# Two cross-attention layers: one maximum and one subtraction a step for the scores of both layers, image scores read from the score tile by ScalarE

## The chip, the cores and the metric

One Trainium2 chip, one core of it. The metric is the device time of one execution, in microseconds (us); the kernel before took 2496.99 us, the median of three runs (2496.69 to 2499.29). Four compute engines work side by side: TensorE (PE, its weight loads are PEld), VectorE (DVE), ScalarE (ACT) and GpSimd (POOL). SyncE (SP) issues most DMAs. TensorE writes its results to PSUM, eight banks; ScalarE and VectorE read them there.

## What is computed

64 sequences of 256 tokens with 320 channels go through two cross-attention layers with 20 heads of 16 channels each. The context has 77 tokens of 512 channels. Layer 0 uses all 77 as text (the reference's image part of layer 0 is over an empty slice). Layer 1 uses the first 73 as text and the last 4 as image tokens:

```python
# layer 0
q, k, v = heads(x @ Wq.T), heads(text @ Wk.T), heads(text @ Wv.T)
x = softmax(q @ k.T * scale) @ v  -> @ Wo.T + bo + x
# layer 1
probs_t = softmax(q @ k_t.T * scale)              # 73 text tokens
attn    = q @ k_ip.T * scale                      # 4 image tokens
qsem    = l2norm(probs_t @ text_ehs)
fused   = attn + 0.5 * (qsem @ l2norm(ip_ehs).T)
ip_out  = (softmax(fused) * mask) @ v_ip
x = (probs_t @ v_t + ip_out) @ W_out + b_out + x
```

A softmax does not change when the same number is taken from all scores of a row, so any number near the maximum may be subtracted. `fused` is shifted by its own maximum later, in `image_shifted`.

## The kernel before

All 64 sequences are taken in 32 pairs p. A pair has ten units of attention in each layer: for each of its two sequences five (part, half) units, each of 128 tokens by eight heads. The main loop goes over steps g; k = g mod 10 is the place in a pair's ten. Step g works on three units at once:

- the scores of layer 0 of unit g and of layer 1 of unit g - 13 (`now[0]`, `now[1]`),
- the transposes of the weights of the units before (`last0`, `last1`),
- layer 1's "semantics" of the unit before that (`before1`): sums over the text with values, Gram matrix and ones.

One PSUM tile `sc` of four banks [128, 4, 512], a single buffer, holds all scores of a step. Each bank has 2 x 77 columns for layer 0, 2 x 77 for layer 1 and, from column 308, 2 x 94 for the semantics. `scores` (L659) and `semantics` (L774, L781) write it. The next step's L774 may begin only when this step's readers are through. Two more PSUM pools have two banks each: `ptr` (tag "tr") for transposes, `pms` (tag "ms") for projections, keys, values, Gram matrices and attention times values. A buffer is taken over when the copy that empties it has ended. These copies are nearly all ScalarE's.

The order of a step, engine by engine, is the order in which the loop issues it (`keep_order` fixes that from step 13 on):

- TensorE: L774, L781, L659; transposes of layer 1 (`tr` L723, `rtr` L724); a filler; transposes of layer 0; more fillers; `attend` (`pv` L809, L814) in steps 0, 2, 5 and 7.
- VectorE: for each layer a maximum (L677) and a subtraction (L679) by `shifted`; `prod` (L792, L795) by `weighted`; the sum (L705) and reciprocal (L706) by `normalize`; `nrm` (L1130).
- ScalarE: copies of what earlier fillers left in PSUM; `pt`, `pr` of layer 1 (L730, L731); the exponential of layer 0 (L687), in step 5 after layer 0's `pt`; the first fillers' copies, such as keys `kT` (L348), values `vs` (L391), Gram (L516, L517), last queries (L589); `pt`, `pr` of layer 0 (L738, L741, L749, L750); the copy of the sums (L1057) by `sums_out`, ahead of layer 0's `pt` in steps 1, 6 and 8; the two exponentials of layer 1 (L690, L691); the second fillers' copies.
- GpSimd: the copy of layer 1's four image scores out of `w` (L694); the normalisation of layer 0 (`parts`, L710); masks and placing.

Fillers that matter here: step 0 the Gram matrix `g_ps`, and `attend`; step 2 `q_ps` L575 and `attend`; step 4 keys `k_ps` and two query tiles `q_ps` (L547); step 5 `k_ps` and `attend`; step 6 a pair of value rows `v_ps`; step 7 `k_ps`, `kl_ps` and the transposes of the image weights `itr` (L915, `image_transposed`), then `attend`; step 8 value rows, then `outputs` with `atr` and `ltr`, of which `ltr` sits in the transposes' pool.

`place_image_keys` (step 6) puts the four image keys behind the 73 text keys of layer 1, in columns 73 to 76; `keys_by_head` spreads keys over a block by head (`kbd`).

Of the kernel before, what the change touches and what calls it, by code (L numbers as in the profile page):

```python
# [8 lines left out]
F32 = mybir.dt.float32  # L9
AF = mybir.ActivationFunctionType  # L10
ALU = mybir.AluOpType
AX = mybir.AxisListType
# [7 lines left out]
T = 77  # L20
NIP = 4
TT = T - NIP
P = 128
KE = E // P
PAD = 32
# [4 lines left out]
GR = GV - M  # L30
R0, R1 = T - M, TT - M
QR = 32
# [38 lines left out]
def tile_two_cross_attentions(ctx: ExitStack, tc: tile.TileContext, a: dict, out: bass.AP):  # L71
# [35 lines left out]
    nc = tc.nc  # L107
# [15 lines left out]
    def load_chan(name, queue):  # L123


        w = const.tile([P, 4, C], F32, tag=name, name=name)
        nc.vector.memset(w[HALF:, 2, :], 0.0)
        nc.vector.memset(w[:HALF, 3, :], 0.0)
        queue.dma_start(w[:, :2, :], a[name][: 2 * P, :].rearrange("(i p) c -> p i c", p=P))
        for b in range(2):  # L130
            queue.dma_start(w[b * HALF : (b + 1) * HALF, 2 + b, :], a[name][2 * P :, :])
        return w

    def load_out(name, queue):
        w = const.tile([P, 4, C], F32, tag=name, name=name)
        nc.vector.memset(w[HALF:, 2, :], 0.0)
# [198 lines left out]
    kTs, kbds, qs, aTs = {}, {}, {}, {}  # L335

    def keys(l, p, i):

        nt = (T, TT)[l]
        if i == 0:  # L340
            kTs[l] = big.tile([P, 2, 2, T], F32, tag=f"kT{l}", name=f"kT{l}_{p}", bufs=1)
        ps = pms.tile([P, 512], F32, tag="ms", name=f"k_ps{l}_{p}_{i}")
        pv = ps[:, : 2 * nt].rearrange("p (b t) -> p b t", b=2)
        for k in range(KE):
            nc.tensor.matmul(  # L345
                pv, wk[l][:, k, i * P : (i + 1) * P], cts[p][:, k, :, :nt], start=(k == 0), stop=(k == KE - 1)
            )
        nc.scalar.copy(kTs[l][:, i, :, :nt], pv)  # L348

    def last_keys(p):  # L350

        ps = pms.tile([P, 512], F32, tag="ms", name=f"kl_ps{p}")
        pv = ps[:, : 2 * T].rearrange("p (b t) -> p b t", b=2)
        for k in range(KE):
            nc.tensor.matmul(pv, wk_last[:, k, :], cts[p][:, k], start=(k == 0), stop=(k == KE - 1))
        for l in range(2):
            nt = (T, TT)[l]
            kl = kls[l, p] = big.tile([P, 2, T], F32, tag=f"kl{l}", name=f"kl{l}_{p}", bufs=1 + l)
            own, other = (slice(h * HALF, (h + 1) * HALF) for h in (l, 1 - l))
            nc.scalar.copy(kl[own, :, :nt], pv[own, :, :nt])  # L360
            nc.sync.dma_start(kl[other, :, :nt], kl[own, :, :nt])

    kls = {}

    def place_image_keys(p):

        k = kipT[:, :, 2 * p * NIP : 2 * (p + 1) * NIP].rearrange("p i (b t) -> p i b t", b=2)
        nc.gpsimd.tensor_copy(kTs[1][:, :, :, TT:], k[:, :2])
        nc.gpsimd.tensor_copy(kls[1, p][:, :, TT:], k[:, 2])

    def keys_by_head(l, p, b):

        kbd = kbds[l, b] = big.tile([P, 3, 2, T], F32, tag=f"kbd{l}", name=f"kbd{l}_{p}_{b}")
        for i, k in ((slice(0, 2), kTs[l][:, :, b, :]), (slice(2, 3), kls[l, p][:, b : b + 1, :])):
            full = [P, k.shape[1], 2, T]
            nc.gpsimd.tensor_tensor(
                kbd[:, i], k.unsqueeze(2).broadcast_to(full),
                head_mask[:, :2].unsqueeze(1).unsqueeze(3).broadcast_to(full), ALU.mult,
            )
# [33 lines left out]
    def values(l, p, b):  # L413

        nt = (T, TT)[l]
        rem = nt - M
# [225 lines left out]
    stats = {}  # L642
    ws, pts = {}, {}

    def eight(t, u):

        return t[:, PLACES[u] : PLACES[u] + 8].rearrange("p (r e) ... -> p r e ...", e=2)

    SEM0 = 4 * T

    def scores(ps, start, stop, l, p, b, u):

        part, s = UNITS[l][u]
        q, kbd, t0 = qs[l, p, part], kbds[l, b], b * S + s * P
        tokens = q[:, b, :] if part == 2 else q[:, t0 : t0 + P]
        for r in range(4):
            rows = slice(r * QR, (r + 1) * QR)
            for c in halves_of(P):
                nc.tensor.matmul(  # L659
                    ps[c, r, 2 * T * l : 2 * T * (l + 1)], tokens[rows, c],  # L660
                    kbd[rows, part].rearrange("p e t -> p (e t)"), start=start, stop=stop,
                )

    def shifted(ps, l, p, b, u):


        nt = (T, TT)[l]
        name = f"{l}_{p}_{b}{u}"
        if l and u == 0:
            stats[p, b] = (  # L670
                small.tile([P, 2 * H, NIP], F32, tag="att", name=f"att{p}_{b}", bufs=3),
                big.tile([P, 2 * H, NIP + D + 1], F32, tag="sums", name=f"sums{p}_{b}", bufs=3),
                small.tile([P, 2 * H], F32, tag="nrm", name=f"nrm{p}_{b}", bufs=3),
            )
        sc = ps[:, :, 2 * T * l : 2 * T * (l + 1)].rearrange("p r (e t) -> p r e t", t=T)
        mx = small.tile([P, 4, 2], F32, tag="mx", name=f"mx{name}")
        nc.vector.tensor_reduce(mx, sc[:, :, :, :nt], AX.X, ALU.max)  # L677
        w = ws[l] = sp.tile([P, 4, 2, T], F32, tag=f"w{l}", name=f"w{name}", bufs=2 - l)
        nc.vector.tensor_tensor(  # L679
            w, sc, mx.unsqueeze(3).broadcast_to([P, 4, 2, T]), ALU.subtract  # L680
        )

    def exponential(l, g, p, b, u):

        w = ws[l]
        if not l:
            nc.scalar.activation(w, w, AF.Exp, scale=SCALE)  # L687
            return
        two = ws[l] = parts1[g % 3]
        nc.scalar.activation(two[:, :4].rearrange("p (e a) j t -> p (a j) e t", e=2), w[:, :, :, :M], AF.Exp, scale=SCALE)  # L690
        nc.scalar.activation(  # L691
            rests(two), w[:, :, :, M:TT], AF.Exp, scale=SCALE
        )
        nc.gpsimd.tensor_copy(eight(stats[p, b][0], u), w[:, :, :, TT:])  # L694

    def rests(two):

# [3 lines left out]
    def normalize(g):  # L701

        w = ws[0]
        sm = small.tile([P, 4, 2], F32, tag="sm", name=f"sm{g}")
        nc.vector.tensor_reduce(sm, w, AX.X, ALU.add)  # L705
        nc.vector.reciprocal(sm, sm)  # L706
        two = ws[0] = sp.tile([P, 8 * T], F32, tag="parts0", name=f"parts0_{g}")
        w, sm = (t.rearrange("p j g ... -> p (j g) ...") for t in (w, sm))
        for t0, t1 in ((0, M), (M, T)):
            nc.gpsimd.tensor_tensor(  # L710
                two[:, 8 * t0 : 8 * t1].rearrange("p (h t) -> p h t", h=8), w[:, :, t0:t1],
                sm.unsqueeze(2).broadcast_to([P, 8, t1 - t0]), ALU.mult,
            )

    def transposed(l, p, b, u, w):
# [47 lines left out]
    def semantics(ps, start, stop, p, b, u, rows):  # L763
# [5 lines left out]
        for i in range(4):  # L769
            for j in range(2):  # L770
                half_rows = slice(j * M, (j + 1) * M)
                at = SEM0 + i // 2 * GV
                for c in halves_of(P):
# [91 lines left out]
    full = [P, 2 * H, NIP]  # L865
# [195 lines left out]
    for g in range(NP * NU + LAG + 12):  # L1061
        p, k = divmod(g, NU)
# [4 lines left out]
        now = [unit(g), unit(g - LAG)]  # L1067
        ps = prod = None
# [5 lines left out]
        if now[0] or now[1] or before1:  # L1074
            ps = psc.tile([P, 4, 512], F32, tag="sc", name=f"sc{g}")
# [6 lines left out]
            for n, (fn, args) in enumerate(todo):  # L1082
                fn(ps, n == 0, n == len(todo) - 1, *args)
        ends = before1 and before1[2] == BU - 1
        for l in range(2):
            if now[l]:
                shifted(ps, l, *now[l])
        if g in middle:
            fn, args = middle.pop(g)
            fn(*args)  # L1090
# [1 line left out]
        if last1:  # L1092
            transposed(1, *last1)
            new1 = (*last1, pts[1])
        if now[0] and k != 5:
            exponential(0, g, *now[0])
        if k == 2:
# [4 lines left out]
        if k != 2:  # L1102
            for fn, args in first:
                fn(*args)
        if before1 and k in (1, 6, 8):
            sums_out(ps)
        if last0:
            transposed(0, *last0)
# [6 lines left out]
            keep_busy(8)  # L1115
        if now[0] and k == 5:
            exponential(0, g, *now[0])
        if before1 and k not in (1, 6, 8):
            sums_out(ps)
        for fn, args in between.pop(g, ()):  # L1120
            fn(*args)
# [6 lines left out]
        if before1:  # L1128
            q, b, u = before1[:3]
# [10 lines left out]
        if last0:  # L1140
            q, b, u, _ = last0
# [9 lines left out]
        before1 = new1  # L1151
# [52 lines left out]
```

## Time and profile before

| | us |
|---|---|
| runs, median (lowest to highest) | 2496.99 (2496.69 to 2499.29) |
| profiled execution, own time | 2497.88 |
| its span, first to last instruction | 2496.2 |
| mean granted TensorE clock | 0.997 |

The costliest groups of VectorE and ScalarE around the change, from the table of groups kept apart by shape:

| line | what | count | mean ns |
|---|---|---|---|
| L677 | maximum, 616 numbers, layer 0 | 320 | 796 |
| L677 | maximum, 584 numbers, layer 1 | 320 | 756 |
| L679 | subtraction, 616 numbers | 640 | 800 |
| L792, L795 | `prod`, 512 and 72 numbers | 320 each | 681, 223 |
| L687 | exponential of layer 0, 616 numbers | 320 | 719 |
| L730 | `pt`, 512 numbers | 320 | 585 |
| L731 | `pr`, 128 numbers | 320 | 273 |
| L1057 | sums, 168 numbers | 320 | 300 |
| L694 | image scores on GpSimd, 32 numbers | 320 | 210 |

In such lines "128x616" is partitions by elements; "x320" counts instructions; the idle time in square brackets or after the bar is the engine's own just before the instruction, with what ended it. A row of the list of waits has the total in us, the number of times and the longest. Printed times of instructions that follow each other on an engine overlap by about 0.1 us, since the next one starts before the last result is written.

### The profile page before, as it was taken

How to read it: one execution, taken by the hardware profiler on the slowest of the kernel's cores; microseconds unless marked ns; L12 is line 12 of the kernel's file. 1: busy time of each engine (PE TensorE's matmuls, PEld its weight loads, DVE VectorE, ACT ScalarE, POOL GpSimd, SP SyncE). 2: the span in 40 equal slices, each digit the busy share in tenths (PEclk: the TensorE clock that was granted, in tenths of full speed). 3: DMA queues.
4: the chain of work that ended last, by engine and by line, in shares of the span. 5: the costliest groups of instructions: out<-in, count | busy, mean ns of one | idle time of the engine just before them, and what ended most of it. 6: DMA issues, size and time to landing. Idle time of an engine off the chain costs nothing.

```text
span 2496.2 us, 100470 instructions
## 1 busy us (share of the span) xinstructions
PE 2401.9 (96%) x41118; PEld 1849.4 (74%) x41118; DVE 1987.1 (80%) x3673; ACT 1479.6 (59%) x3767; POOL 1371.7 (55%) x3483
## 2 busy tenths in 40 slices
PE   8899999999999999999999999999999999999888
PEld 5677777777777777777777777777777777777666
DVE  3588888888887888888888888888887888888764
ACT  3465666665665665665665666665665666666543
POOL 2456555556555656555555555555555556555542
PEclk9999999999999999999999999999999999999999
DMA  5212111112211121211111211111211111211000
GB/s 172 75 30 58 55 53 47 48 53 60 59 47 46 48 58 56 61 45 46 48 58 55 63 43 50 44 58 55 63 43 50 44 58 55 61 39 39 26 23 25
DMA packets 150914, 131.83 MB, mean 53 GB/s; under 512 B 45432, under 2 KB 129144, under 8 KB 150456
## 3 DMA queue, kind: packets, MB, share of 16 engines
q1 hardware_dynamic: 149592, 124.27, 17.2%
q8 instruction: 325, 5.32, 0.9%
q10 hardware_dynamic: 864, 1.15, 0.2%
q14 instruction: 133, 1.09, 0.1%
HBM read 87.43 MB, written 33.91 MB: 49 GB/s over the span
## 4 chain that ended last, share of the span: by engine, by line
PE 75%; DVE 15%; ACT 4%; DMA 2%; issue 2%; POOL 1%; SPq 0%; DVEq 0%; POOLq 0%; ACTq 0%
PE sc L774 9%; PE tr L723 9%; PE o_ps L547 8%; PE q_ps L547 8%; PE sc L659 7%; DVE w L679 6%; DVE mx L677 4%; PE sc L781 4%; PE o_ps L632 3%; PE k_ps L345 3%; PE pv L809 3%; PE v_ps L390 2%; PE o_ps L557 2%; DVE prod L792 2%; PE q_ps L557 2%; PE q_ps L575 2%
## 5 line engine op out<-in xcount | busy, mean ns | idle before, releaser
L677 DVE TENSOR_REDUCE mx<-sc 128x8 f32<-128x584 f32 (+1 forms) x640 | 496.9, 776 | 365.1 <-PE sc L659 362.2
L710 POOL TENSOR_TENSOR parts<-w,sm 128x512 f32<-128x512 f32 (+1 forms) x640 | 440.5, 709 | 459.8 <-DVE sm L706 184.0
L679 DVE TENSOR_TENSOR w<-sc,mx 128x616 f32<-128x616 f32 x640 | 512.0, 800 | 73.0 <-DVE mx L677 0.9
L723 PE MATMUL tr<-ident,parts 128*128 128x128 f32 x2560 | 408.1, 282 | 9.5 <-ACT pt L730 5.6
L723 PEld LDWEIGHTS tr<-ident,parts 128*128 128x128 f32 x2560 | 284.7, 141 | 128.7 <-issue 83.2
L730 ACT COPY pt<-tr 128x512 f32<-128x512 f32 x320 | 187.1, 585 | 322.4 <-PE tr L723 317.4
L687 ACT ACTIVATE w<-w 128x616 f32<-128x616 f32 x320 | 230.2, 719 | 142.4 <-DVE w L679 138.4
L774 PEld LDWEIGHTS sc<-gv,pt 64*64 64x64 f32 x10240 | 233.1, 133 | 105.5 <-ACT sums L1057 52.7
L774 PE MATMUL sc<-gv,pt 64*64 64x94 f32 x10240 | 277.3, 245 | 23.6 <-ACT sums L1057 23.0
L694 POOL COPY att<-w 128x32 f32<-128x32 f32 x320 | 67.0, 210 | 356.6 <-DVE w L679 352.9
L705 DVE TENSOR_REDUCE sm<-w 128x8 f32<-128x616 f32 x320 | 251.0, 784 | 14.4 <-ACT w L687 14.2
L659 PE MATMUL sc<-kbd,q 32*64 32x154 f32 x10240 | 247.7, 293 | 1.1 <-ACT q L602 1.0
L1057 ACT COPY sums<-sc 128x168 f32<-128x168 f32 x320 | 96.2, 300 | 245.0 <-DVE prod L795 245.0
L547 PE MATMUL q_ps<-x,wq 128*128 128x256 f32 x1024 | 232.7, 380 | 5.3 <-ACT kT L348 5.3
L547 PE MATMUL o_ps<-aT,wo 128*128 128x256 f32 x1024 | 231.8, 379 | 0.7 <-ACT aT L945 0.7
L1130 DVE TENSOR_REDUCE nrm<-prod 128x8 f32<-128x584 f32 x320 | 226.8, 709 | 0.3
L792 DVE TENSOR_TENSOR prod<-sc,parts 128x512 f32<-128x512 f32 x320 | 217.9, 681 | 2.8 <-PE sc L781 2.8
L547 PEld LDWEIGHTS q_ps<-x,wq 128*128 128x128 f32 x1024 | 189.2, 190 | 29.9 <-ACT kT L348 6.9
L547 PEld LDWEIGHTS o_ps<-aT,wo 128*128 128x128 f32 x1024 | 189.6, 190 | 24.5 <-ACT aT L945 1.2
L690 ACT ACTIVATE parts<-w 128x512 f32<-128x512 f32 x320 | 207.0, 647 | 0.0
L749 ACT COPY pt<-tr 128x512 f32<-128x512 f32 x256 | 150.6, 588 | 66.4 <-PE tr L723 65.3
L390 PE MATMUL v_ps<-wv,cf 128*128 128x320 f32 (+1 forms) x624 | 179.2, 433 | 0.0
(144 smaller groups left out, 4566.2 us busy)
## 6 DMA issues: line engine op xcount, KB each, us to landing
out_dram<-x SPq DMA_DIRECT2D x64, 256.0 KB
x<-in_x_dram SPq DMA_DIRECT2D x31, 512.0 KB
v_rows<-vs SPq DMA_DIRECT2D x38, 320.0 KB
vm<-v_rows SPq DMA_DIRECT2D x152, 80.0 KB
ct<-in_ctx_dram SPq DMA_DIRECT2D x32, 308.0 KB
cf<-in_ctx_dram SPq DMA_DIRECT2D x38, 256.0 KB
g_rest<-gram_rest SPq DMA_DIRECT2D x512, 0.5 KB
v_rest<-v_rows SPq DMA_DIRECT2D x448, 11.2 KB
```

What stands on the lines that cost most here:

```text
L390: nc.tensor.matmul(ps[:n, :C], cfs[i][:, k, :n], wv[l][:, k, :], start=(k == 0), stop=(k == KE - 1))
L547: nc.tensor.matmul(ps[b][:, m, :], w[:, k, m * P : (m + 1) * P], main[:, k, b * S : (b + 1) * S], start=(k == 0 and m == 0), stop=False,)
L659: nc.tensor.matmul(ps[c, r, 2 * T * l : 2 * T * (l + 1)], tokens[rows, c], kbd[rows, part].rearrange("p e t -> p (e t)"), start=start, sto ...
L677: nc.vector.tensor_reduce(mx, sc[:, :, :, :nt], AX.X, ALU.max)
L679: nc.vector.tensor_tensor(w, sc, mx.unsqueeze(3).broadcast_to([P, 4, 2, T]), ALU.subtract)
L687: nc.scalar.activation(w, w, AF.Exp, scale=SCALE)
L705: nc.vector.tensor_reduce(sm, w, AX.X, ALU.add)
L710: nc.gpsimd.tensor_tensor(two[:, 8 * t0 : 8 * t1].rearrange("p (h t) -> p h t", h=8), w[:, :, t0:t1], sm.unsqueeze(2).broadcast_to([P, 8, ...
L723: nc.tensor.transpose(ps[:, i, :], flat[:, i * P : (i + 1) * P], ident)
L774: nc.tensor.matmul(ps[c, i % 2 * 2 + j, at : at + GV], pt[half_rows, i, c], gv[b][half_rows, part, i, :], start=start and i < 2, stop=False,)
L792: nc.vector.tensor_tensor(prod[:, :, :, :M], sm[:, :, :, :M], w[:, :4].rearrange("p (e a) j t -> p (a j) e t", e=2), ALU.mult)
L1130: nc.vector.tensor_reduce(eight(stats[q, b][2], u), prod, AX.X, ALU.add)
```

## The change

Layer 1's keys get 81 columns: the 73 text keys, a second copy of the first four text keys in columns 73 to 76, and the four image keys in columns 77 to 80. So a head of layer 1 has a row of 77 text scores like layer 0, whose maximum is that of the 73, and behind it the plain image scores. In the score tile every head has 81 columns, 4 x 81 + 2 x 94 = 512.

- `shifted` issues one maximum and one subtraction over the 4 heads of a bank (two of each layer) by 77 columns, where both layers have a unit; the result `w` is one tile with two buffers instead of `w0` with two and `w1` with one.
- The image scores aren't copied out of `w` by GpSimd after layer 1's exponentials; `image_scores_out`, on ScalarE, copies them, not shifted, from columns 77 to 80 of the score tile, after layer 1's `pt` and `pr` and ahead of layer 0's exponential.
- `place_image_keys` issues four small copies on GpSimd instead of two; the two that double text keys read what ScalarE's key copies (L348, L360) and the DMA between the halves of `kl` have written.
- `sums_out` comes behind layer 0's `pt` and `pr` in step 8 too.

```diff
+TK = T + NIP
...
-        nc.gpsimd.tensor_copy(kTs[1][:, :, :, TT:], k[:, :2])
-        nc.gpsimd.tensor_copy(kls[1, p][:, :, TT:], k[:, 2])
+        for to, image in ((kTs[1], k[:, :2]), (kls[1, p], k[:, 2])):
+            nc.gpsimd.tensor_copy(to[..., T:], image)
+            nc.gpsimd.tensor_copy(to[..., TT:T], to[..., :NIP])
...
-        kbd = kbds[l, b] = big.tile([P, 3, 2, T], F32, tag=f"kbd{l}", name=f"kbd{l}_{p}_{b}")
+        n = (T, TK)[l]
+        kbd = kbds[l, b] = big.tile([P, 3, 2, n], F32, tag=f"kbd{l}", name=f"kbd{l}_{p}_{b}")
...
-    SEM0 = 4 * T
+    SEM0 = 4 * TK
...
-                    ps[c, r, 2 * T * l : 2 * T * (l + 1)], tokens[rows, c],
-                    kbd[rows, part].rearrange("p e t -> p (e t)"), start=start, stop=stop,
+                    by_head_block(ps)[c, r, 2 * l : 2 * l + 2, : kbd.shape[3]], tokens[rows, c], kbd[rows, part],
+                    start=start, stop=stop,
...
-        sc = ps[:, :, 2 * T * l : 2 * T * (l + 1)].rearrange("p r (e t) -> p r e t", t=T)
-        mx = small.tile([P, 4, 2], F32, tag="mx", name=f"mx{name}")
-        nc.vector.tensor_reduce(mx, sc[:, :, :, :nt], AX.X, ALU.max)
-        w = ws[l] = sp.tile([P, 4, 2, T], F32, tag=f"w{l}", name=f"w{name}", bufs=2 - l)
-        nc.vector.tensor_tensor(
-            w, sc, mx.unsqueeze(3).broadcast_to([P, 4, 2, T]), ALU.subtract
-        )
+        h0, h1 = (0 if now[0] else 2), (4 if now[1] else 2)
+        full = [P, 4, h1 - h0, T]
+        sc = by_head_block(ps)[:, :, h0:h1, :T]
+        mx = small.tile([P, 4, 4], F32, tag="mx", name=f"mx{g}")[:, :, h0:h1]
+        w = sp.tile([P, 4, 4, T], F32, tag="w", name=f"w{g}")
+        nc.vector.tensor_reduce(mx, sc, AX.X, ALU.max)
+        nc.vector.tensor_tensor(w[:, :, h0:h1], sc, mx.unsqueeze(3).broadcast_to(full), ALU.subtract)
+        for l in range(2):
+            ws[l] = w[:, :, 2 * l : 2 * l + 2]
+
+    def image_scores_out(ps, p, b, u):
+        nc.scalar.copy(eight(stats[p, b][0], u), by_head_block(ps)[:, :, 2:, T:])
...
-        nc.gpsimd.tensor_copy(eight(stats[p, b][0], u), w[:, :, :, TT:])
...
-        for l in range(2):
-            if now[l]:
-                shifted(ps, l, *now[l])
+        if now[0] or now[1]:
+            shifted(ps, g, now)
...
+        if now[1]:
+            image_scores_out(ps, *now[1])
         if now[0] and k != 5:
             exponential(0, g, *now[0])
...
-        if before1 and k in (1, 6, 8):
+        if before1 and k in (1, 6):
             sums_out(ps)
...
-        if before1 and k not in (1, 6, 8):
+        if before1 and k not in (1, 6):
             sums_out(ps)
```

Here `by_head_block(ps)` is the first 4 x 81 columns of each bank, seen as head by column.

More of the change, by code (lines that the diff above doesn't have):

```diff
@@ L340, in keys @@
         if i == 0:
-            kTs[l] = big.tile([P, 2, 2, T], F32, tag=f"kT{l}", name=f"kT{l}_{p}", bufs=1)
+            kTs[l] = big.tile([P, 2, 2, (T, TK)[l]], F32, tag=f"kT{l}", name=f"kT{l}_{p}", bufs=1)
         ps = pms.tile([P, 512], F32, tag="ms", name=f"k_ps{l}_{p}_{i}")
@@ L357, in last_keys @@
             nt = (T, TT)[l]
-            kl = kls[l, p] = big.tile([P, 2, T], F32, tag=f"kl{l}", name=f"kl{l}_{p}", bufs=1 + l)
+            kl = kls[l, p] = big.tile([P, 2, (T, TK)[l]], F32, tag=f"kl{l}", name=f"kl{l}_{p}", bufs=1 + l)
             own, other = (slice(h * HALF, (h + 1) * HALF) for h in (l, 1 - l))
@@ L367, in place_image_keys @@
         k = kipT[:, :, 2 * p * NIP : 2 * (p + 1) * NIP].rearrange("p i (b t) -> p i b t", b=2)
-        nc.gpsimd.tensor_copy(kTs[1][:, :, :, TT:], k[:, :2])
-        nc.gpsimd.tensor_copy(kls[1, p][:, :, TT:], k[:, 2])
+        for to, image in ((kTs[1], k[:, :2]), (kls[1, p], k[:, 2])):
+            nc.gpsimd.tensor_copy(to[..., T:], image)
+            nc.gpsimd.tensor_copy(to[..., TT:T], to[..., :NIP])
     def keys_by_head(l, p, b):
-        kbd = kbds[l, b] = big.tile([P, 3, 2, T], F32, tag=f"kbd{l}", name=f"kbd{l}_{p}_{b}")
+        n = (T, TK)[l]
+        kbd = kbds[l, b] = big.tile([P, 3, 2, n], F32, tag=f"kbd{l}", name=f"kbd{l}_{p}_{b}")
         for i, k in ((slice(0, 2), kTs[l][:, :, b, :]), (slice(2, 3), kls[l, p][:, b : b + 1, :])):
-            full = [P, k.shape[1], 2, T]
+            full = [P, k.shape[1], 2, n]
             nc.gpsimd.tensor_tensor(
@@ L659, in scores, with by_head_block, shifted @@
                 nc.tensor.matmul(
-                    ps[c, r, 2 * T * l : 2 * T * (l + 1)], tokens[rows, c],
-                    kbd[rows, part].rearrange("p e t -> p (e t)"), start=start, stop=stop,
-                )
[L664 to L669, printed above, removed]
+                    by_head_block(ps)[c, r, 2 * l : 2 * l + 2, : kbd.shape[3]], tokens[rows, c], kbd[rows, part],
+                    start=start, stop=stop,
+                )
+    def by_head_block(ps):
+        return ps[:, :, : 4 * TK].rearrange("p r (h t) -> p r h t", t=TK)
+    def shifted(ps, g, now):
+        if now[1] and now[1][2] == 0:
+            p, b = now[1][:2]
             stats[p, b] = (
@@ L707, in normalize @@
         two = ws[0] = sp.tile([P, 8 * T], F32, tag="parts0", name=f"parts0_{g}")
-        w, sm = (t.rearrange("p j g ... -> p (j g) ...") for t in (w, sm))
         for t0, t1 in ((0, M), (M, T)):
             nc.gpsimd.tensor_tensor(
-                two[:, 8 * t0 : 8 * t1].rearrange("p (h t) -> p h t", h=8), w[:, :, t0:t1],
-                sm.unsqueeze(2).broadcast_to([P, 8, t1 - t0]), ALU.mult,
+                two[:, 8 * t0 : 8 * t1].rearrange("p (j g t) -> p j g t", j=4, g=2), w[:, :, :, t0:t1],
+                sm.unsqueeze(3).broadcast_to([P, 4, 2, t1 - t0]), ALU.mult,
             )
```

## The prediction

> **What bounds the kernel now.** The page first. TensorE is 96% busy and the chain that ended last runs 75% on it; the score matmuls, semantics and projections follow each other with few holes. VectorE's 15% of the chain is the second thing to look at.
>
> ```profile
> PE 2401.9 (96%) x41118; PEld 1849.4 (74%) x41118; DVE 1987.1 (80%) x3673; ACT 1479.6 (59%) x3767; POOL 1371.7 (55%) x3483
> ...
> PE 75%; DVE 15%; ACT 4%; DMA 2%; issue 2%; POOL 1%; SPq 0%; DVEq 0%; POOLq 0%; ACTq 0%
> ```
>
> A share over the span hides that the loop has ten kinds of step (k = g mod 10). I therefore took the start of each step (the first L774 matmul after a pause) and its length by k, from the timeline. Typical lengths, k = 5 to 9 and then 0 to 4: 6.21, 6.47, 6.79, 8.17, 7.46, 7.20, 7.28, 7.06, 8.88, 8.22 us. In 6 of 31 groups of ten a second pair of value rows falls into step 6 and 8, which are then 8.2 and 9.4. Times below are from a step's start. Only two steps end on VectorE: in 5 and 6 the next L774 waits for the sums' copy on ScalarE, which waits for `prod`. The other eight end on TensorE's own work. The list of waits shows who holds whom:
>
> ```profile
> ACT sums L1057 <- DVE prod L795: 245.0, 267, 3.4
> ...
> ACT w L687 <- DVE w L679: 138.4, 258, 3.7
> ...
> PEld pv L809 <- ACT gram_rest L517: 6.1, 29, 0.6
> ```
>
> The third row (total, times, longest) is small, but it comes 29 times: in step 0 TensorE's `pv` starts on the very end of a ScalarE copy. So ScalarE, 59% busy, has places without slack. Step 7, first VectorE, then ScalarE, then TensorE (start, length):
>
> ```profile
> 1094.03 0.80 DVE L677 TENSOR_REDUCE mx<-sc 128x8 f32<-128x616 f32 x1
> 1094.86 0.80 DVE L679 TENSOR_TENSOR w<-sc,mx 128x616 f32<-128x616 f32 x1
> 1095.58 0.76 DVE L677 TENSOR_REDUCE mx<-sc 128x8 f32<-128x584 f32 x1
> 1096.47 0.80 DVE L679 TENSOR_TENSOR w<-sc,mx 128x616 f32<-128x616 f32 x1
> 1097.18 0.68 DVE L792 TENSOR_TENSOR prod<-sc,parts 128x512 f32<-128x512 f32 x1
> 1097.78 0.22 DVE L795 TENSOR_TENSOR prod<-sc,parts 128x72 f32<-128x72 f32 x1
> ```
> ```profile
> 1095.75 0.72 ACT L687 ACTIVATE w<-w 128x616 f32<-128x616 f32 x1 [0.43 <-DVE w L679]
> 1096.38 0.27 ACT L348 COPY kT<-k_ps 128x154 f32<-128x154 f32 x1
> 1096.54 0.59 ACT L749 COPY pt<-tr 128x512 f32<-128x512 f32 x1
> ```
> ```profile
> 1096.02 1.22 PE L355 MATMUL kl_ps<-ct,wk_last 128*128 128x154 f32 x8
> 1097.18 0.83 PE L915 MATMUL itr<-ident,iw 128*80 128x128 f32 x4
> ```
>
> The reader is to see: layer 0's exponential (L687) starts as soon as the first `w` is there, 1.72 us after the first maximum; the `pt` copy behind it ends at 1097.13, and `itr`, which takes over that PSUM buffer, starts at 1097.18 with no hole in TensorE. Step 0 is the same with the Gram copies:
>
> ```profile
> 1118.97 0.72 ACT L687 ACTIVATE w<-w 128x616 f32<-128x616 f32 x1
> 1119.59 0.19 ACT L516 COPY gram<-g_ps 64x64 f32<-64x64 f32 x1
> 1119.69 0.16 ACT L517 COPY gram_rest<-g_ps 73x13 f32<-73x13 f32 x1
> ```
> ```profile
> 1119.90 0.64 PE L809 MATMUL pv<-pt,v 128*32 128x256 f32 x8
> ```
>
> **VectorE's part.** Two maxima and two subtractions over 616 (584) numbers become one of each over 1232. L792 (512 numbers, 681 ns) and L795 (72, 223 ns) give 1.04 ns a number and 0.15 us fixed. So 800 ns + 616 x 1.04 = 1.44 us each. The two maxima's rows (756 ns for 584, 796 for 616) would say 1.25 ns, so 1.57; that is the dear end, 1.40 the cheap one (fixed part read 0.04 too low). I take 1.44, whose two rows lie farther apart. Four instructions of 3.15 us become two of 2.88, and one handoff goes: the last score is shifted about 0.3 us earlier. The first is shifted 1.3 us later, and both layers' exponentials wait for it.
>
> **The copy of the image scores** (L694, 210 ns on GpSimd, 320 times) goes to ScalarE, reads PSUM and stands ahead of layer 0's exponential. Nearest rows: 64x64 0.19, 73x13 0.16, 128x128 0.27; I take 0.19, bounds 0.16 and 0.27. ScalarE's next instruction starts some 0.10 before a printed end, so its slot is 0.09. In the program as built it waits for the subtraction, and `prod` waits for it: 0.08 + 0.19 + 0.05 give back nearly all of the 0.3 us on VectorE. `prod` starts about where it did; behind it stand the sum, its reciprocal and `nrm`, then GpSimd's `parts`, which the next step's transposes need 1.2 us later or more. GpSimd's 67 us were free: nothing on TensorE waited for L694.
>
> That reads of one bank are ordered between engines is in this trace already: the sums' copy waits for `prod` in 267 cases, though they read other columns. The Trainium skill, "PSUM — Partial Sum Buffer", section "PSUM bank collisions raise a hardware error", gives the reason: two engines must not touch the same bank and 32 partitions at once, reads by ScalarE and VectorE included. It speaks against this move. If it didn't hold, the copy could run while VectorE works, the delay below would be 0.09 less, and the sum some 14 us lower (5 steps x 30).
>
> **The delay on ScalarE.** Exponential of layer 0, from the first maximum's start: before 1.72 to 1.80; after 1.44 + 0.05 + 1.44 + 0.08 + 0.09 = 3.10. So 1.38 us later in each step, with all that is queued behind it on ScalarE: kT, q, Gram, value and `pt` copies, which free PSUM buffers for TensorE. What each step has of slack, by the rows:
> Step 7: `pt` end to `itr` is 0.05, a bare handoff: loss 1.37.
> Step 0: Gram rest's end (1119.85) to `pv` 0.05: loss 1.38.
> Step 2: `pt` waited for TensorE 0.25 and `pv` came 0.38 after it was ready: loss 1.38 - 0.63 = 0.75.
> Step 4: the kT copy ends at 4.45, the second q tile, which needs its buffer, begins at 5.49: 0.99 free, loss 0.39.
> Step 5: there the exponential already stood last, but the new copy now stands ahead of kT and `pt`. Copy 4.82, kT 4.91, `pt` 5.08, `pr` 5.56, exponential 5.72, sums 6.35 to 6.65, next step 6.71: loss 0.50.
> Steps 1 and 9: `pt` waits for TensorE until 6.36, the exponential ends at 5.7: none. Step 3: the q copy ends at 5.92, its buffer is needed at 6.14: none.
> Step 6 (24 groups): `prod` started at 5.27 behind `most`; now 4.87 + 0.19 + 0.05 = 5.11: gain 0.16.
> Step 8 (24 groups): `ltr` waited for `pt`, which stood behind the sums' copy until 6.09. With the sums' copy moved behind, exponential, value copy and `pt` end at 6.50 and `ltr` starts at 6.55 instead of 6.74: gain 0.19. Without the move `pt` would end near 6.8.
>
> **The small rest.** Layer 1's scores widen from 154 to 162 columns: half of L659's 0.56 us in the chain by 5% is 0.015 us in 305 steps, 4.5 us. Keys by head grow 5% on GpSimd and two small copies per pair are added (0.2 us each by the rows of their twins; they wait for the kT copy, which in step 7 ends at 1.69, while GpSimd comes to them at 2.10). This lies beside idle time; bounds 0 and 32 x 0.4 = 13 us if GpSimd were late, I take 0, as `parts` ends 1.2 us or more ahead of its transposes in steps 6 and 7. The last eleven steps have no layer 0: `prod` comes 0.25 us later in five short ones, 1.2 us. The first thirteen keep their work. Buffers of `w` are free earlier than layer 1's were (one before, two now): it doesn't bind.
>
> **Sum.** 30 groups x (1.37 + 1.38 + 0.75 + 0.39 + 0.50) = 131.7; less 24 x 0.35 = 8.4; plus 5.7: 129 us. The profiled execution took 2497.88 (span 2496.2), 0.9 above the median of 2496.99: so 2627.
>
> **Rivals.** (a) Only the two steps without slack lose (0 and 7), the others absorb: 30 x 2.75 = 83, 2580. For it: the slacks of 2, 4 and 5 rest on modelled ends. Against: their copies' order is fixed. Anything down to no change goes with it. (b) Dearer: 1.57 us for both instructions, 0.26 more delay: 5 x 0.26 x 30 + the gains lost, 47 us: 2674. A fall of the granted clock would add to it; the trace has TensorE waits of 2.2 us (`ltr`) at a mean clock of 0.997, and the new ones are 1.4. (c) Faster: VectorE's shorter shift decides. Place: the end of steps 5 and 6, where the sums' copy ends last; price 0.2 to 0.3 us x 55 steps, 11 to 17 us, so 2483. It decides only if the exponential's delay stays within the slack of steps 0 and 7, about 0.05 us, so if the one subtraction ended hardly later than the first of two does: against 1.38 from the rows. The program as built has one subtraction that all wait for, so that the change doesn't do what it says is out.
>
> **How the numbers follow.** Forecast 0.70, (b) beyond 2680 0.08, (a) below 2580 but slower 0.16, (c) and no change 0.06. Range 2580 to 2680, from (a)'s end to a little over (b)'s. What can be told from no change here is 0.2%, 5 us: faster 0.04, same 0.02, slower 0.94.
>
> **What would show it.** Right: the exponential of layer 0 starts 3.1 us after the maximum; steps 7 and 0 near 8.2 and 8.6 us, step 2 near 7.8, step 5 near 6.7, step 6 near 6.3; `itr`, `pv` and q matmuls waiting for ScalarE. Wrong: steps 7 and 0 at their old length, a maximum or subtraction far from 1.44, or a copy of the image scores that ends before the subtraction.

## The result and the profile after

The changed kernel takes 2605.94 us, the median of four runs (2605.67 to 2607.6), against 2496.84 (2496.39 to 2499.29) for the kernel before beside it: a ratio of 1.0436, 95% interval 1.0418 to 1.0454. The direction was forecast, and the time lies in the range; the loss of 109 us is 20 us smaller than the forecast's.

The profiled execution has a span of 2604.1 us at a mean granted TensorE clock of 0.998 (0.997 before), so the clock has no part in it. First and fourth part of its page, busy time by engine and the chain that ended last:

```profile
PE 2412.2 (93%) x41118; PEld 1845.5 (71%) x41118; DVE 1960.4 (75%) x3059; ACT 1480.8 (57%) x4087; POOL 1318.9 (51%) x3227
...
PE 44%; DVE 37%; ACT 8%; issue 5%; DMA 2%; SPq 1%; POOL 1%; ACTq 0%; DVEq 0%; POOLq 0%
```

VectorE has 614 instructions and 27 us of work less, and ScalarE's busy time has grown by only 1.2 us. Yet the chain that ended last left TensorE, whose share went from 75% to 44%, and VectorE's went from 15% to 37%. Less work, and more of it in the way. The table of groups, kept apart by shape (busy us, mean ns; idle before, with what ended it), shows that the prices of single instructions were as forecast or close:

```profile
L685 DVE TENSOR_TENSOR w<-sc,mx 128x1232 f32<-128x1232 f32 x307 | 442.6, 1442 | 28.4 <-DVE mx L684 0.9
L684 DVE TENSOR_REDUCE mx<-sc 128x16 f32<-128x1232 f32 x307 | 441.6, 1438 | 414.2 <-PE sc L662 410.7
...
L662 PE MATMUL sc<-kbd,q 32*64 32x162 f32 x5120 | 162.8, 300 | 0.3 <-ACT q L605 0.2
L662 PE MATMUL sc<-kbd,q 32*64 32x154 f32 x5120 | 152.1, 294 | 0.8 <-ACT q L605 0.8
```

Two instructions of 1.44 us take the place of four (the forecast's figure); eight more columns cost a matmul 6 ns, 2% where 5% was forecast. The list of waits (total, times, longest) shows the new ones and those that grew:

```profile
ACT att L690 <- DVE w L685: 505.4, 318, 3.8
...
DVE prod L799 <- ACT att L690: 57.4, 224, 1.2
...
PEld pv L816 <- ACT gram_rest L520: 45.3, 29, 1.6
PEld itr L922 <- ACT pt L756: 43.9, 30, 2.5
...
PEld pv L816 <- ACT pt L756: 30.9, 32, 1.5
```

The first row is the delay itself: ScalarE, which waited 138.4 us for its first `w` before, now waits 505.4 us for the one late subtraction, in 318 of 320 cases with the copy of the image scores, as forecast. That ScalarE idles costs nothing; what stands behind it in its queue is late. This shows in the three rows on PEld: TensorE waits 1.0 to 1.6 us at a time (45.3 / 29, 43.9 / 30, 30.9 / 32) for ScalarE copies that have nothing to do with scores. The first of them was 6.1 us before. The timeline of one step 7 (it begins at 1141.21; start, length) shows the link:

```profile
1143.03 1.44 DVE L684 TENSOR_REDUCE mx<-sc 128x16 f32<-128x1232 f32 x1
1144.51 1.44 DVE L685 TENSOR_TENSOR w<-sc,mx 128x1232 f32<-128x1232 f32 x1
1146.20 0.69 DVE L799 TENSOR_TENSOR prod<-sc,parts 128x512 f32<-128x512 f32 x1 [0.25 <-ACT att L690]
...
1145.98 0.18 ACT L690 COPY att<-sc 128x32 f32<-128x32 f32 x1 [1.59 <-DVE w L685]
1146.07 0.72 ACT L696 ACTIVATE w<-w 128x616 f32<-128x616 f32 x1
1146.68 0.28 ACT L349 COPY kT<-k_ps 128x154 f32<-128x154 f32 x1
1146.85 0.60 ACT L756 COPY pt<-tr 128x512 f32<-128x512 f32 x1
...
1145.09 1.22 PE L356 MATMUL kl_ps<-ct,wk_last 128*128 128x154 f32 x8
1147.50 0.64 PE L922 MATMUL itr<-ident,iw 128*80 128x128 f32 x4 [1.20 <-ACT pt L756]
```

VectorE ends the one subtraction 4.74 us into the step; ScalarE, idle for 1.59 us, then copies the image scores, starts layer 0's exponential at 4.86 and reaches `pt` at 5.64. `itr` takes over `pt`'s PSUM buffer, and TensorE stands still for 1.20 us. ScalarE is 57% busy and still makes TensorE wait, since the copy comes behind the exponential in its order: the transposes that `pt` copies had ended at 1145.14, 1.7 us before the copy began.

### The profile page after: what moved, and what is told of

Its sections match the earlier page's. It is cut to its first block, busy times and chain, and to the rows that moved or that the text cites. A ratio compares the mean times of both kernels' runs of the same rounds, so it can differ in the third digit from the quotient of the medians.

```text
span 2604.1 us, 99832 instructions
## 1 busy us (share of the span) xinstructions
PE 2412.2 (93%) x41118; PEld 1845.5 (71%) x41118; DVE 1960.4 (75%) x3059; ACT 1480.8 (57%) x4087; POOL 1318.9 (51%) x3227
## 4 chain that ended last, share of the span: by engine, by line
PE 44%; DVE 37%; ACT 8%; issue 5%; DMA 2%; SPq 1%; POOL 1%; ACTq 0%; DVEq 0%; POOLq 0%
DVE w L685 14%; DVE mx L684 13%; PE sc L781 7%; PE q_ps L550 6%; PE sc L662 5%; DVE x L620 3%; PE sc L788 3%; PE pv L816 3%; PE tr L730 3%; PE v_ps L393 3%; PE q_ps L560 2%; ACT w L696 2%; DVE sm L713 2%; PE pv L821 2%; DVE nrm L1138 2%
## 5 line engine op out<-in xcount | busy, mean ns | idle before, releaser
L684 DVE TENSOR_REDUCE mx<-sc 128x16 f32<-128x1232 f32 (+1 forms) x333 | 462.1, 1388 | 464.5 <-PE sc L662 461.0
L685 DVE TENSOR_TENSOR w<-sc,mx 128x1232 f32<-128x1232 f32 (+1 forms) x333 | 463.4, 1392 | 30.2 <-DVE mx L684 0.9
L737 ACT COPY pt<-tr 128x512 f32<-128x512 f32 x320 | 187.1, 585 | 366.9 <-PE tr L730 365.9
L690 ACT COPY att<-sc 128x32 f32<-128x32 f32 x320 | 59.3, 185 | 505.4 <-DVE w L685 505.4
L799 DVE TENSOR_TENSOR prod<-sc,parts 128x512 f32<-128x512 f32 x320 | 220.8, 690 | 61.8 <-ACT att L690 57.4
L662 PE MATMUL sc<-kbd,q 32*64 32x154 f32 (+1 forms) x10240 | 252.4, 297 | 1.1 <-ACT q L605 1.0
L550 PE MATMUL q_ps<-x,wq 128*128 128x256 f32 x1024 | 239.9, 382 | 5.2 <-ACT kT L349 4.8
L699 ACT ACTIVATE parts<-w 128x512 f32<-128x512 f32 x320 | 213.0, 666 | 0.0
L731 PE MATMUL rtr<-ident,parts 128*104 128x128 f32 (+1 forms) x640 | 174.6, 273 | 0.0
L662 PEld LDWEIGHTS sc<-kbd,q 32*64 32x64 f32 x10240 | 168.7, 132 | 6.3 <-issue 5.1
```

The source lines that it names most:

```text
L550: nc.tensor.matmul(ps[b][:, m, :], w[:, k, m * P : (m + 1) * P], main[:, k, b * S : (b + 1) * S], start=(k == 0 and m == 0), stop=False,)
L662: nc.tensor.matmul(by_head_block(ps)[c, r, 2 * l : 2 * l + 2, : kbd.shape[3]], tokens[rows, c], kbd[rows, part], start=start, stop=stop,)
L684: nc.vector.tensor_reduce(mx, sc, AX.X, ALU.max)
L685: nc.vector.tensor_tensor(w[:, :, h0:h1], sc, mx.unsqueeze(3).broadcast_to(full), ALU.subtract)
L799: nc.vector.tensor_tensor(prod[:, :, :, :M], sm[:, :, :, :M], w[:, :4].rearrange("p (e a) j t -> p (a j) e t", e=2), ALU.mult)
```

## The experiments

Eight kernels were run, four and four, each four beside the kernel before on one chip. For each I took the length of every step and the start of layer 0's exponential from the step's start. Typical values (medians by k over the regular groups, us), worked out from the timelines:

```
                      step lengths                                          start of layer 0's exponential
                       0    1    2    3    4    5    6    7    8    9        0    2    4    5    7
before               7.20 7.28 7.06 8.88 8.22 6.20 6.47 6.78 8.17 7.46     4.39 3.58 3.56 4.88 3.59
after                8.57 7.29 7.65 8.89 8.66 6.68 6.28 7.86 7.94 7.47     5.77 4.81 4.88 5.69 4.86
merged_behind        8.31 7.29 7.63 8.89 8.64 5.97 6.25 7.84 7.92 7.51     5.50 4.79 4.86 4.80 4.84
split_ahead          9.10 7.29 8.10 9.06 8.92 6.94 6.54 8.12 8.20 7.47     6.29 5.26 5.14 5.95 5.12
split_behind         7.09 7.29 7.07 8.89 8.24 6.23 6.51 6.97 7.24 7.51     4.28 3.54 3.58 4.81 3.55
one_max_two_subs     7.54 7.29 7.07 8.89 8.23 6.04 6.31 7.21 7.28 7.51     4.73 4.15 4.22 4.62 4.21
merged_behind_late   7.35 7.29 7.07 8.89 8.24 5.98 6.25 6.95 7.24 7.51     6.11 5.10 4.86 4.80 4.84
before_sums8         7.26 7.28 7.06 8.88 8.22 6.20 6.47 6.80 7.22 7.46     4.45 3.58 3.56 4.88 3.60
before_wide          7.20 7.29 7.07 8.89 8.23 6.21 6.49 7.05 8.19 7.47
merged_in_5_6        7.09 7.29 7.07 8.89 8.24 5.97 6.25 6.56 7.24 7.51     4.28 3.51 3.58 4.81 3.55
```

**Which of the two parts: four kernels in a square.** One kernel leaves the merged instructions and puts the copy of the image scores behind the sums; one splits the instructions by layer again and leaves the copy ahead of the exponential; one does both. The copy behind:

```diff
-        if now[1]:
-            image_scores_out(ps, *now[1])
         if now[0] and k != 5:
             exponential(0, g, *now[0])
...
-        if before1 and k in (1, 6):
-            sums_out(ps)
+        if k in (1, 6):
+            if before1:
+                sums_out(ps)
+            if now[1]:
+                image_scores_out(ps, *now[1])
```

The split, in place of the one maximum and subtraction:

```diff
...
         for l in range(2):
-            ws[l] = w[:, :, 2 * l : 2 * l + 2]
+            if now[l]:
+                sc = by_head_block(ps)[:, :, 2 * l : 2 * l + 2, :T]
+                mx = small.tile([P, 4, 2], F32, tag="mx", name=f"mx{l}_{g}")
+                nc.vector.tensor_reduce(mx, sc, AX.X, ALU.max)
+                w = ws[l] = sp.tile([P, 4, 2, T], F32, tag=f"w{l}", name=f"w{l}_{g}")
+                nc.vector.tensor_tensor(w, sc, mx.unsqueeze(3).broadcast_to([P, 4, 2, T]), ALU.subtract)
```

> The changed kernel with the copy of the image scores moved on ScalarE from ahead of layer 0's exponential to behind the sums' copy. Theory (the late exponential holds ScalarE's queue): the exponential starts 0.1 us earlier than in the changed kernel, so steps 0, 2, 4 and 7 lose only 0.1 us less (8.48, 7.55, 8.56, 7.77); step 5, where the copy stood ahead of the key copy, falls from 6.68 to about 5.95; 2567 us. Rival 1 (the copy and its two waits are the cost, the merged VectorE instructions are not): within 15 us of 2497. Rival 2 (the work itself, wider scores and longer instructions): 2606.

> The changed kernel with a maximum and a subtraction per layer again (separate tiles), the copy of the image scores still ahead of layer 0's exponential. Theory: the copy waits for the second subtraction, which ends 0.32 us later than the one of 1232 numbers, and the exponential waits behind the copy: steps 0, 2, 4, 5, 7 each 0.3 us longer than in the changed kernel, steps 6 and 8 too, 2672 us, although the merging is undone. Rival 1: the copy is as before, so 2606. Rival 2: VectorE's work is that of the kernel before, 2500.

> Both undone: a maximum and a subtraction per layer, and the copy of the image scores on ScalarE behind the sums' copy; wide keys and the sums' later place in step 8 stay. Theory: the exponential is back at 1.75 us after the first maximum, all losses gone; the later sums copy of step 8 gives about 0.7 us in 24 of 31 groups, the copy's slot behind the sums costs 0.1 in steps 5 and 6, the wide scores 4: 2489 us. Rival 1: the same, about 2490. Rival 2: 2606 less VectorE's share, about 2590.

Measured: merged_behind 2574.67 us, 1.0303 (1.0287 to 1.0318); split_ahead 2679.21, 1.0722 (1.0704 to 1.074); split_behind 2478.85, 0.9919 (0.9905 to 0.9934). Undoing both gives everything back and more, moving the copy alone gives 31 us, and splitting alone makes it 73 us worse. The theory's forecasts were 2567, 2672 and 2489: right in order, and off by 7 to 10 us. (split_behind's gain over the kernel before is nearly all step 8's, 22.6 us summed over the run where about 17 were forecast; it is taken up below. Its step 7 stays at 6.97, since `itr` waits for something else there, below too.) The start of ScalarE's queue explains why the split helps with the copy behind, by 96 us, and harms with the copy ahead, by 73. With the copy ahead, the exponential waits for VectorE's last subtraction in both cases, and two split pairs end later than the merged one. Timeline of a step 7 of split_ahead (begins at 1173.33), exponential 5.11 us into the step:

```profile
1178.36 0.18 ACT L688 COPY att<-sc 128x32 f32<-128x32 f32 x1 [1.85 <-DVE w L685]
1178.44 0.72 ACT L694 ACTIVATE w<-w 128x616 f32<-128x616 f32 x1
```

The same of merged_behind (begins at 1126.59); VectorE, then ScalarE, then TensorE:

```profile
1129.89 1.44 DVE L685 TENSOR_TENSOR w<-sc,mx 128x1232 f32<-128x1232 f32 x1
...
1131.42 0.72 ACT L696 ACTIVATE w<-w 128x616 f32<-128x616 f32 x1 [1.66 <-DVE w L685]
1132.05 0.27 ACT L349 COPY kT<-k_ps 128x154 f32<-128x154 f32 x1
1132.21 0.59 ACT L756 COPY pt<-tr 128x512 f32<-128x512 f32 x1
...
1132.86 0.63 PE L922 MATMUL itr<-ident,iw 128*80 128x128 f32 x4 [1.18 <-ACT pt L756]
```

And of split_behind (begins at 1087.18), where the exponential needs only layer 0's subtraction and starts after 3.56 us:

```profile
1089.85 0.80 DVE L685 TENSOR_TENSOR w<-sc,mx 128x616 f32<-128x616 f32 x1
...
1090.74 0.72 ACT L694 ACTIVATE w<-w 128x616 f32<-128x616 f32 x1 [0.37 <-DVE w L685]
1091.36 0.27 ACT L349 COPY kT<-k_ps 128x154 f32<-128x154 f32 x1
1091.53 0.59 ACT L754 COPY pt<-tr 128x512 f32<-128x512 f32 x1
```

In merged_behind the copy is gone from ahead of the exponential, and in steps 2, 4 and 7 this still starts only 0.02 us earlier than in the changed kernel (4.84 against 4.86 in step 7), not 0.09: from the subtraction's printed end to the exponential are 0.09 us (1131.33 to 1131.42, and 1090.65 to 1090.74 in split_behind), to the copy in the changed kernel 0.03 (1145.95 to 1145.98). In these steps the copy filled a gap that is there anyway. The 31 us come from elsewhere, as the row of merged_behind shows: summed over the run, step 5 (6.68 to 5.97) gives 20.7 and step 0 (8.57 to 8.31) 7.7. In step 5 layer 0's exponential stands behind the second `pt`, and the copy no longer holds the copies ahead of it.

**A middle dose.** One maximum for both layers, then a subtraction for each, copy behind: the exponential starts 0.6 us late instead of 1.3.

```diff
-        nc.vector.tensor_tensor(w[:, :, h0:h1], sc, mx.unsqueeze(3).broadcast_to(full), ALU.subtract)
...
         for l in range(2):
-            ws[l] = w[:, :, 2 * l : 2 * l + 2]
+            if now[l]:
+                w = ws[l] = sp.tile([P, 4, 2, T], F32, tag=f"w{l}", name=f"w{l}_{g}")
+                nc.vector.tensor_tensor(
+                    w, by_head_block(ps)[:, :, 2 * l : 2 * l + 2, :T],
+                    mx[:, :, 2 * l : 2 * l + 2].unsqueeze(3).broadcast_to([P, 4, 2, T]), ALU.subtract,
+                )
```

> A middle dose: one maximum for both layers, two subtractions (layer 0 first), the copy of the image scores behind the sums' copy. Layer 0's exponential then starts near 4.2, between 3.55 (split_behind) and 4.84 (merged_behind). Theory (delay against each step's own slack): step 0 about 7.7, step 7 about 7.2, steps 2 and 4 at their floor of 7.07 and 8.24, 2498 us. Rival (halfway in work is halfway in time between 2479 and 2575): 2527, steps 2 and 4 at half of their loss.

Measured: 2492.94, 0.9971 (0.996 to 0.9982). Steps 2 and 4 are at their old lengths, 0 and 7 are longer: slack is used up step by step, as the forecast had it, though step 0 is 0.16 us shorter than forecast. (In the profiled execution, which took 3.3 us more than the median, 5.4 us more than in the kernel before lie ahead of the first regular step, 119.3 against 113.9; why stays open.) The table gives more: where the exponential decides, step length less its start is a constant.

```
step 0:  2.81 before, 2.81 split_behind, 2.81 one_max, 2.81 merged_behind, 2.80 after, 2.81 split_ahead
step 2:  2.84 merged_behind, 2.84 after, 2.84 split_ahead; else at its own 7.07
step 4:  3.78 merged_behind, 3.78 after, 3.78 split_ahead; else at its own 8.23
step 7:  3.00 one_max, 3.00 merged_behind, 3.00 after, 3.00 split_ahead, 3.01 merged_in_5_6
```

So these steps run on one rule over all doses from 3.55 to 6.29 us, as long as the order of the queue stays: the exponential's start plus the queue behind it, or the step's own TensorE work, whichever is longer.

**Take the exponential out of the way, merged instructions kept.** Made from merged_behind: in steps 0, 2, 4, 7 and 8 the exponential is issued behind the copies that free PSUM, as step 5 has it already.

```diff
-        if now[0] and k != 5:
+        if now[0] and k not in (0, 2, 4, 5, 7, 8):
             exponential(0, g, *now[0])
...
-        if now[0] and k == 5:
+        if now[0] and k in (0, 2, 4, 5, 7, 8):
```

> The merged instructions kept, the copy of the image scores behind the sums' copy, and layer 0's exponential behind layer 0's pt and pr in steps 0, 2, 4, 5, 7, 8 (in the changed kernel in step 5 alone). Theory: nothing that TensorE needs stands behind the exponential any more; steps 0, 2, 4, 7 back to 7.21, 7.07, 8.25, 6.75, step 5 at 6.0, step 6 at 6.2, step 8 at 7.45: 2472 us, under the kernel before. Rival 1: no better than merged_behind. Rival 2: 2606.

Measured: 2478.48, 0.9917 (0.9902 to 0.9932), 96 us below merged_behind, with the same VectorE instructions, and 6 above the forecast. In step 0 the exponential starts at 6.11, later than in the changed kernel, and the step takes 7.35 instead of 8.57. Timeline of such a step (begins at 1550.11), ScalarE, then TensorE, whose `pv` follows its transposes with no hole:

```profile
1554.39 0.17 ACT L520 COPY gram_rest<-g_ps 73x13 f32<-73x13 f32 x1
...
1556.22 0.73 ACT L696 ACTIVATE w<-w 128x616 f32<-128x616 f32 x1
...
1555.58 0.64 PE L816 MATMUL pv<-pt,v 128*32 128x256 f32 x8
```

So it is not the exponential that is needed early; it is what stands behind it. Step 7 came down to 6.95, not 6.75, since `itr` waits for GpSimd as in split_behind. Step 0 did not come down to split_behind's 7.09: VectorE reaches the first maximum 0.28 us later. One small instruction ahead of it is long there, beside a GpSimd instruction:

```profile
1549.95 0.24 DVE L877 TENSOR_TENSOR least<-sums 128x40 f32<-128x40 f32 x1
1550.23 1.01 DVE L878 SCALAR_TENSOR_TENSOR nrm<-least,nrm 128x40 f32<-128x40 f32 x1
...
1550.14 1.37 POOL L717 TENSOR_TENSOR parts<-w,sm 128x512 f32<-128x512 f32 x2
```

In split_behind the same two take 0.71 and 0.26 us, beside an earlier `parts`. In both kernels the long one ends 0.06 to 0.10 us after the first of GpSimd's two `parts` (medians over 30 steps). That GpSimd's work holds it was not tested apart.

**Step 8's sums alone**, on the kernel before.

```diff
-        if before1 and k in (1, 6, 8):
+        if before1 and k in (1, 6):
...
-        if before1 and k not in (1, 6, 8):
+        if before1 and k not in (1, 6):
```

> The kernel before with one thing of the change: in step 8 the sums' copy stands behind layer 0's pt and pr. Theory: pt no longer waits for prod, ltr starts when TensorE comes to it, near 6.0 instead of 6.74; step 8 falls from 8.17 to 7.24 in 24 of 31 groups, 2475 us, and all other steps stay. Rival (the move pays only together with the late exponential): step 8 falls by 0.2 at most, 2493.

Measured: 2475.86, 0.9903 (0.9889 to 0.9916); step 8 goes from 8.17 to 7.22. Timeline of a step 8 of the kernel before (begins at 1098.95), TensorE and ScalarE:

```profile
1103.92 1.04 PE L928 MATMUL atr<-ident,an 128*128 128x128 f32 x8
1105.69 0.44 PE L928 MATMUL ltr<-ident,an_last 128*128 128x128 f32 x2 [0.73 <-ACT pt L749]
...
1104.85 0.30 ACT L1057 COPY sums<-sc 128x168 f32<-128x168 f32 x1 [0.85 <-DVE prod L795]
1105.04 0.59 ACT L749 COPY pt<-tr 128x512 f32<-128x512 f32 x1
```

And of before_sums8 (begins at 1091.94):

```profile
1096.91 1.04 PE L928 MATMUL atr<-ident,an 128*128 128x128 f32 x8
1097.78 0.38 PE L928 MATMUL ltr<-ident,an_last 128*128 128x128 f32 x2
...
1097.00 0.59 ACT L749 COPY pt<-tr 128x512 f32<-128x512 f32 x1
...
1097.84 0.30 ACT L1057 COPY sums<-sc 128x168 f32<-128x168 f32 x1
```

The sums wait for `prod` and made `pt` wait, 6.09 us into the step; without them it starts at 5.06 and `ltr` follows `atr` with no hole. So in the kernel before, step 8 too ended on VectorE, by way of the sums and `pt`. In the changed kernel the late exponential takes most of this back (step 8 at 7.94). By the spans the rest of the change therefore costs 2604.1 - 2473.2 = 131 us, and this one edit, worth 23 alone, hides a part of it.

**Wider keys alone**, on the kernel before: 81 columns, the image keys placed twice (four GpSimd copies), the extra columns written and read by nobody.

```diff
-        nc.gpsimd.tensor_copy(kTs[1][:, :, :, TT:], k[:, :2])
-        nc.gpsimd.tensor_copy(kls[1, p][:, :, TT:], k[:, 2])
+        nc.gpsimd.tensor_copy(kTs[1][:, :, :, TT:T], k[:, :2])
+        nc.gpsimd.tensor_copy(kTs[1][:, :, :, T:], k[:, :2])
+        nc.gpsimd.tensor_copy(kls[1, p][:, :, TT:T], k[:, 2])
+        nc.gpsimd.tensor_copy(kls[1, p][:, :, T:], k[:, 2])
...
```

> The kernel before with 81 key columns in layer 1 and four placing copies on GpSimd instead of two (the extra columns hold the image keys once more and are read by nobody); the rest as before. Theory: 0.013 us a step for the wider score matmuls, 4 us, and in step 7 the image weights come 0.2 to 0.35 us later on GpSimd, so itr ends later by 0.17, 5 us: 2506. Rival 2 (wider scores are the main cost of the change): over 2550.

Measured: 2508.58, 1.0034 (1.0021 to 1.0047). Summed by k, the other kinds of step change by -0.1 to 0.4 us each over the whole run; step 7 costs 6.8 (6.78 to 7.05 a step). Its timeline (begins at 1098.06):

```profile
1103.08 0.76 POOL L869 TENSOR_TENSOR iw<-num,imx 128x64 f32<-128x64 f32 x3
...
1103.12 1.08 PE L922 MATMUL itr<-ident,iw 128*80 128x128 f32 x4
```

`itr` is 1.08 us long, 0.63 where it has nothing to wait for: its four parts follow the image weights `iw`, which GpSimd makes meanwhile. The copies put GpSimd's queue back: `iw` starts 5.02 us into this step, 4.74 in the kernel before (1096.89, below). In the changed kernel this is free, since `itr` starts after `iw` is ready and takes 0.64; the cover is the loss itself.

**A version that beats both.** split_behind, with the merged instructions only in steps 5 and 6, which end on VectorE, and GpSimd's image values moved from step 6 to step 7, behind `iw`. (`w` is one tile for both layers here, layer by layer inside.)

```diff
+        one_go = g % NU in (5, 6) and now[0] and now[1]
...
+        if one_go:
+            nc.vector.tensor_reduce(mx, sc, AX.X, ALU.max)
+            nc.vector.tensor_tensor(
...
-            for b in range(2):
-                add(1, p - 2, place_image_values, b)
...
+            for b in range(2):
+                add(0, p - 2, place_image_values, b)
```

> split_behind with one maximum and one subtraction in steps 5 and 6 alone, whose end waits for VectorE, and with the masks on the image values (place_image_values) issued behind the image weights in step 7 instead of in step 6. Theory: steps 5 and 6 at 5.97 and 6.25 instead of 6.23 and 6.51, step 7 at 6.6 instead of 6.97 as itr no longer waits for GpSimd; about 25 us under split_behind, 2454. Rival 1 (the merged instructions gain nothing anywhere): no change in 5 and 6.

Measured: 2454.44, 0.9816 (0.9802 to 0.9829), 45 us below the kernel before beside it and 151 below the changed one. Steps 5 and 6 have the merged lengths (5.97, 6.25 against 6.23, 6.51 split), and step 7 is at 6.56, since `iw` is ready long before `itr`. Its timeline (begins at 1075.87):

```profile
1078.70 0.76 POOL L878 TENSOR_TENSOR iw<-num,imx 128x64 f32<-128x64 f32 x3
...
1080.86 0.64 PE L931 MATMUL itr<-ident,iw 128*80 128x128 f32 x4
```

## Why the forecast was right, and 20 us too high

The mechanism is shown: in the square, the middle dose and the kernel with the late exponential, the steps move as the start and the order of ScalarE's queue say. Of the rivals, (a) is out, since steps 2, 4 and 5 lose too; (b) is out, since both instructions take 1.44; (c)'s gain is real (steps 5 and 6, 0.26 each) but small, and decides only where the delay is kept away, as in merged_in_5_6. The forecast added its loss to the profiled execution, not to the median, which is 0.9 of the 20 us. The sum, by its terms (predicted, then from the two traces, in us over all groups):

| term | predicted | measured | a typical step |
|---|---|---|---|
| step 7 | 41.1 | 34.3 | +1.08, not 1.37 |
| step 0 | 41.4 | 40.3 | +1.37, forecast 1.38 |
| step 2 | 22.5 | 18.0 | +0.59, not 0.75 |
| step 4 | 11.7 | 7.2 | +0.44, forecast 0.39 |
| step 5 | 15.0 | 12.3 | +0.48, forecast 0.50 |
| steps 6 and 8 | -8.4 | -7.8 | -0.19 and -0.23, forecast -0.16 and -0.19 |
| steps 1, 3, 9, start and tail | 5.7 | 3.7 | +0.01 |
| sum | 129 | 108 | |

- **The delay, forecast as 1.38 us for every step, was too dear in most.** From the first maximum to the exponential were 1.72 to 1.73 us before in steps 0, 2 and 7 and 1.80 in step 4 (medians); after, 3.09, 3.02, 3.03 and 3.10. That is 1.30 us more in steps 2, 4 and 7, and 1.36 in step 0. From the subtraction's printed end to the exponential are 0.11 us by the medians (0.12 in the rows above), not the forecast 0.08 + 0.09. The first maximum itself moves too: 0.07 earlier in step 2, 0.02 earlier in step 7, 0.01 to 0.02 later in steps 0 and 4. Together: 1.23 in step 2, 1.27 in step 7, 1.32 in step 4, and only in step 0 the forecast's 1.38.
- **Step 7 was mis-sized, by 6.8 us.** I read "`pt` ends at 1097.13, `itr` starts at 1097.18" as no slack. But `itr` took 0.83 us there and takes 0.64 now: it waited inside for `iw`, which GpSimd was still making. In the kernel before:

```profile
1096.89 0.76 POOL L862 TENSOR_TENSOR iw<-num,imx 128x64 f32<-128x64 f32 x3
```

By the constant, the old step would have been 3.59 + 3.00 = 6.59 without that, and it was 6.78: 0.19 us of slack in a row that looked like plain work. So the loss is 1.27 - 0.19 = 1.08, not 1.37; 0.19 of the difference is this slack, 0.10 the delay.

- **Step 2, 4.5 us:** the slack that I read, 0.63, was right to 0.01; the delay of 1.23 makes the difference.
- **Step 4, 4.5 us:** the typical step lost a little more than forecast, and that it came so close was in part luck: the delay was 0.06 too dear, but the slack was 0.88 by the constant (8.22 - 3.56 - 3.78), not 0.99. That the total is below the forecast comes from four groups, whose step 4 took 9.65 to 10.05 us before; none does after. In these four, GpSimd waits 4.7 to 5.1 us for value rows that a DMA brings (`vm`, in one of the four `v_rest`), the keys by head (`kbd`) come late, ScalarE's key copy waits 2.2 to 2.6 us for them, and TensorE's second query tile 1.2 to 1.6 us for that copy. In the changed kernel such a wait for rows in step 4 is 3.7 us at most (3.3 for `vm`), and the key copy no longer waits for `kbd`. The rows of the two lists of waits, before and after:

```profile
POOL v L464 <- DMA vm<-v_rows: 21.7, 6, 5.1
...
ACT kT L348 <- POOL kbd L376: 10.5, 6, 2.6
```
```profile
POOL v L467 <- DMA vm<-v_rows: 17.4, 8, 3.3
```

- **Step 5:** 30 steps lost 0.48; the last two, in the tail, became 2.2 us shorter together (9.18 to 8.46, 7.88 to 6.35), which the sum has in it.
- **The copy of the image scores.** Its length was right (185 ns against 0.19). `prod` waits for it 224 times, 57.4 us in all, and this takes back what the merging had gained, as forecast: in step 7 `prod` starts at 5.00 us, 5.02 before and 4.66 in merged_behind. The price in step 5 was forecast (0.50); in steps 2, 4 and 7 the copy delays the exponential by 0.02 us, not 0.09; in step 0, by 0.27 (5.50 to 5.77), since the first maximum also comes 0.18 later than in merged_behind.
- **GpSimd's four copies at nothing:** right in the changed kernel. The bound of 13 us for the lost cover held too: 6.8.
- **Step 8's move:** the +0.19 was worked out for the changed kernel and held (0.23). What it would be worth alone, 0.95 us a step, wasn't asked. The prediction's "the other eight end on TensorE's own work" does not fit its own rows here: step 8 ended on `ltr`, which waited for `pt`, and step 0 on ScalarE's queue (the constant 2.81 holds before the change as well).

## What to carry to other kernels

An instruction that serves two readers at once makes the first reader wait for the whole of it. Before you merge, look at what is queued behind that reader on its own engine; here, with the copy of the image scores behind in both, merging took 48 us of work from VectorE (1997.1 to 1949.1) and cost 96 us (2478.85 to 2574.67), because the exponential held copies that free PSUM. The copy ahead of the exponential cost another 31. Merge in the stages that end on the merging engine, and elsewhere move the waiting instruction behind the copies that others need. And before you call a handoff slackless, compare the length of the instruction after it with its undisturbed length: an instruction that waits inside hides slack.

## What was not expected of the hardware

From the printed end of a VectorE subtraction to the start of the ScalarE instruction that waits for it, the trace nearly always has one of two values: 0.034 us or 0.094 us. In the kernel before, the exponential of layer 0 has the first in 66 of its 258 waits and the second in 192. In the 192 (nearly all in steps 2, 3, 4, 7, 8 and 9) the trace has a semaphore instruction of ScalarE's own, 0.017 us long, just ahead of the exponential, which there waits for two semaphores; in the 66 (nearly all in steps 1 and 6) it has none. The copy in the changed kernel waits for one semaphore and has 0.033 us in 317 of 318 cases, with the exponential 0.08 behind its start. So it cost the exponential 0.02 us where the old handoff was 0.094, and 0.08, nearly its own slot, where it was 0.034.

And matmuls that wait between their parts are printed as one longer group (`itr` 0.64, 0.83 and 1.08 us for the same four), with no idle time beside it: in the step 7 shown, their starts are 0.11 to 0.14 us apart in the changed kernel and up to 0.26 in the kernel before, while each is printed as 0.27 to 0.31 us long.
